# Four block sums of a second graph-attention projection, made by GpSimd instead of VectorE

## The chip, the cores and the metric

The kernel runs on one core of one Trainium2 chip. TensorE (PE in the profile) multiplies matrices, VectorE (DVE), ScalarE (ACT) and GpSimd (POOL) do the elementwise work, SyncE (SP) starts DMAs, and GpSimd starts those DMAs that add to what lies at their destination. Each engine works through its own queue in order; semaphores tie the queues together. The metric is the device time of one execution in microseconds (us).

## The reference

Two layers of graph attention with a residual, over 32 graphs of 512 nodes and 512 features:

```python
h = jnp.maximum(_layernorm(x, axis=-1), 0.0)
x = x + _L0_gnn_ref(adj, h, ...)

def gat_layer(x, mask, W, a_src, a_dst, bias, concat):
    xl = (x @ W).reshape(B, N, H, F)
    asrc = jnp.einsum('bnhf,hf->bnh', xl, a_src)
    adst = jnp.einsum('bnhf,hf->bnh', xl, a_dst)
    e = jax.nn.leaky_relu(asrc[:, :, None, :] + adst[:, None, :, :], NEG_SLOPE)
    e = jnp.where(mask[..., None], e, NEG_INF)
    attn = jax.nn.softmax(e, axis=1)
    out = jnp.einsum('bsdh,bshf->bdhf', attn, xl)
    ...
h = jax.nn.elu(gat_layer(x, mask, W1, ..., concat=True))    # 4 heads of 256
h = gat_layer(h, mask, W2, ..., concat=False)               # 1 head of 512
```

The matter here is the second layer's `x @ W2`: for each graph a product of 512 x 1024 with 1024 x 512 (and two more columns for the attention scores).

## The kernel before

Everything is float32. Each of the large products is made by Winograd's form of Strassen's method: both operands are cut into 2 x 2 blocks, a few sums of blocks are made, seven block products take the place of eight, and their results are added up on the way out of TensorE's banks (PSUM). `sums` (line 1008) makes the sums of the left operand:

- s1 = a21 + a22
- a21 = a11 - a21, written over the block a21
- s2 = s1 - a11
- s4 = a12 - s2

The products take their left operands from the table `left`: product 1 from a11, 2 from a12, 3 from s4, 4 from a22, 5 from s1, 6 from s2, 7 from the new a21.

For the second projection the left operand is `h1`, the output of the first layer, transposed: 8 tiles of 128 features by 512 nodes. `h1_blocks` (line 1039) cuts it with kh = KH = 4, so that a block is four 128 x 256 pieces, and each sum is one instruction on 128 partitions x 1024 elements. s1 and s2 go to the two halves of the buffer `hs`; there s4 has no place of its own and is written over s2. So in this case `sums` emits only the first three and leaves the fourth in `left[0]`; `sevens` (line 1058), which runs the seven products, calls it after the last product 6, the reader of s2. The other users of `sums` are the first projection (`ht_blocks`, kh = KQ = 2) and the last product of the second layer (`sums2`, line 1449, kh = KQ); they make sums of 128 x 512.

Product 5, 6 and so on are each made twice, once for each half of 128 rows. The order of `project2` (line 1399) is the table TWO: 1, 1, 2, 5, 6, 6, 2, 5, 7, 7, 3, 3, 4, 4, with the halves mixed.

`hs` is shared. Its first two of four pieces hold the sums of the first projection, the last two those of the last product of the second layer (`gather2`) and, one piece a head, those of the first layer's attention (`sums1`). Each `sums` for `h1` therefore has to wait until these have been read.

The main loop (line 1611) runs over 31 turns. A turn interleaves the work of several graphs: the attention product of the first layer of graph i+1, the first projection of graph i+2, the last product of graph i, and the second projection of graph i+1 with its four sums; one more set of these sums stands before the loop. So there are 32 sets, 128 instructions.

The order of the instructions on every engine is written by a planner, the class `Program` (line 223). The kernel's functions add jobs with an engine, a cost in us and the keys that they read and write. `order` (line 299) then goes through a modelled time: on each engine it takes the ready job of the lowest rank. A job's rank comes from the table PLACES by the job's number, moved on by a fixed amount each turn; it does not depend on the job's engine. On the queues that start DMAs (SP and POOL) a job, of any kind, is held back in the plan while the modelled backlog of transfers is over 3.5 us. On the chip each engine then follows the planned order, and semaphores make it wait where the plan was wrong.

GpSimd's queue holds, besides a few instructions at the start, the accumulating DMAs that add the mask to the attention scores (`accumulate`, line 522; two issues for each attention matrix, each for half of it) and one small power for the layer norm of a graph (line 770). ScalarE's exponential follows these DMAs, and the attention product on TensorE follows the exponential.

Of the kernel before, what the change touches and what calls it, by code (L numbers as in the profile page):

```python
# [378 lines left out]
def tile_gat(  # L379
# [36 lines left out]
    nc = tc.nc  # L416
# [12 lines left out]
    KH = FT // 2  # L429
# [81 lines left out]
    prog = Program()  # L511
# [4 lines left out]
    def dve(cost, reads, writes, f, *a, **k):  # L516
        prog.add("DVE", cost, reads, writes, lambda: f(*a, **k))  # L517

    def dma(size, reads, writes, to, at, cost=0.4):
        prog.add("SP", cost, reads, writes, lambda: nc.sync.dma_start(to, at), size)  # L520

# [85 lines left out]
    def weights1():  # L607
        for c in range(2):
            for r in range(2):
                for k in range(KQ):  # L610
                    row = (r * KQ + k) * P
                    ix = AT[r, c]
                    dma(
                        WLOAD, (), [("w1", ix, k)], w1_sb[:, ix, k, :, 2:],
                        w1[row : row + P, :].rearrange("p (j c f) -> p c j f", j=H // 2, c=2)[:, c],
                    )

    def scores1():

        vk, bc = ps_.take()  # L620
        for a, v in enumerate((as1, ad1)):
            for j in range(H // 2):
                dma(
                    XLOAD, (), [vk + ("v", a, j)], bc[:, 2 * a + j, :],
                    bass.AP(tensor=v.tensor, offset=v.offset + j * 2 * FH, ap=[[0, P], [1, 2 * FH]]),
                )
        for j in range(H // 2):
            for c in range(2):
                for a in range(2):
                    for r in range(2):  # L630
                        for k in range(KQ):
                            ix = AT[r, c]
                            jk, junk = xrs.take()
                            dve(
                                0.4, [vk + ("v", a, j), ("w1", ix, k)], [("w1s", ix, k, j), jk],
                                nc.vector.scalar_tensor_tensor,
                                junk[:, :FH], w1_sb[:, ix, k, j, 2:], 1.0,
                                bc[:, 2 * a + j, c * FH : (c + 1) * FH],
                                op0=OP.mult, op1=OP.mult, accum_out=w1_sb[:, ix, k, j, a : a + 1],
                            )  # L640
                            xrs.give(jk)
        for u in range(NT):
            for c in range(2):
                prog.alias(vk + (u, c), [vk + ("v", a, j) for a in range(2) for j in range(H // 2)])
        ps_.give(vk)

    def weights2():

        for (r, c), ix in AT.items():
            dma(  # L650
                2 * WLOAD, [("ht", 0, 0)], [("w2", ix)], w2_sb[:, ix, :, :M],
                w2[r * HF // 2 : (r + 1) * HF // 2, c * DO // 2 : (c + 1) * DO // 2].rearrange(
                    "(k p) f -> p k f", p=P
                ),
            )
# [342 lines left out]
    def hs_keys(i, k0, k1):  # L998
        return [("hs", i, k) for k in ((0,) if k0 == 0 else ()) + tuple(range(max(k0, KQ), k1))]
# [8 lines left out]
    def sums(blocks, kh, cost, at=0, place=None, keys=None):  # L1008

        a11, a12, a21, a22 = (blocks[r, c] for r, c in ((0, 0), (0, 1), (1, 0), (1, 1)))  # L1010
        if place is None:
            s1, s2 = ((hs[:, i, at : at + kh], hs_keys(i, at, at + kh)) for i in range(2))
            s4 = (hs4, [("hs", 2, 0), ("hs", 2, 1)]) if kh == KQ and at == 0 else s2
        else:
            s1, s2, s4 = (
                (place[:, i].rearrange("p (k m) -> p k m", m=M), keys) for i in range(3)
            )

        def op(f, to, u, v):
            dve(cost, u[1] + v[1], to[1], f, to[0], u[0], v[0])  # L1020

        op(nc.vector.tensor_add, s1, a21, a22)
        op(nc.vector.tensor_sub, a21, a11, a21)
        op(nc.vector.tensor_sub, s2, s1, a11)
        left = {1: a11, 2: a12, 3: s4, 4: a22, 5: s1, 6: s2, 7: a21}

        def last():
            op(nc.vector.tensor_sub, s4, a12, s2)

        if s4 is s2:  # L1030
            left[0] = last
        else:
            last()
        return left
# [414 lines left out]
    def sums2(b, soft, place=None, keys=None):  # L1449

        pk, p = soft.p[0]
        blocks = half_blocks(p, KQ, lambda r, c: p_keys(pk, (2 * c, 2 * c + 1), (r,)))
        left = sums(blocks, KQ, 0.602, KQ, place, keys)
        v = x2(b)
        b11, b12, b21, b22 = (
            (
                v[:, 2 * r : 2 * r + 2, c * W2H : (c + 1) * W2H],
                [x2_key(b, 2 * r + i, c) for i in range(2)],
            )
            for r in range(2) for c in range(2)  # L1460
        )
        t1, t2, t4 = (
            (t.rearrange("p (k f) -> p k f", f=M + 1), [k]) for k, t in (xs.take() for _ in range(3))
        )
        dve(TINY, (), t1[1], nc.vector.memset, t1[0][:, :, M:], 1.0)

        def op(to, a, c):
            dve(
                0.602, a[1] + c[1], to[1], nc.vector.tensor_sub,
                *(q[0][:, :, :M] for q in (to, a, c)),  # L1470
            )

        op(t1, b12, b11)
        op(t2, b22, t1)
        op(b12, b22, b12)
        op(t4, b21, t2)
        right = {1: b11, 2: b21, 3: b22, 4: t4, 5: t1, 6: t2, 7: b12}
        return left, {n: (q if n in (1, 2, 5) else q[:, :, :M], keys) for n, (q, keys) in right.items()}
# [91 lines left out]
    for n in SMALL:  # L1570
        sums_of_small_weights(n)
    left1 = sums(ht_blocks(), KQ, 0.602)
    s = S1[0] = Soft(0, 1, lambda z, i, zk: [zk + (0, c, t) for c in range(2) for t in range(NT)])
    for i in range(2):
# [27 lines left out]
    s.first(3)  # L1602
    sums_of_weights(w2_sb, lambda ix: [("w2", ix), ("w2s", ix)], 1.15)
    left2 = sums(h1_blocks(), KH, 1.135)
    run(project2(0, left2))
    for t in range(NT):
# [103 lines left out]
```

## Time and profile before

| | us |
|---|---|
| median of two runs | 2766.11 (2766.06 to 2766.17) |
| span of the profiled execution | 2767.6 |
| TensorE busy | 2742.4 |
| VectorE busy | 2558.2 |
| ScalarE busy | 2229.1 |
| GpSimd busy | 313.1 |

"Busy" counts the time in which at least one of the engine's instructions ran; instructions of one engine overlap a little, so one of 1.22 us on VectorE is followed by the next after 1.13. In a row of groups stand the line, the engine, the operation, the output and the inputs by their names, the shapes and the count, then the busy time, the mean of one in ns, and the idle time just before them with what ended it. A row of the timeline has the start in us from the start of the span, the length in us, then the same names; with "x8" the row holds eight instructions in a row. Line 531 is every matmul, 517 every VectorE instruction and 514 every ScalarE one, since helpers emit them; one tells them apart by the names. A 32-bit matmul shows as two rows, so one product of the second projection (four matmuls) has eight. A row "A <- B: 12.1, 1, 12.1" of the waits says that A waited for B for 12.1 us in all, once, 12.1 at the longest.

### The profile page before, as it was taken

The page shows a single profiled execution, that of the slowest core. Times are in us where ns is not written, and L with a number is a line of the kernel's source. Part 1 is how long each engine was busy: PE and PEld are TensorE (multiplying, and loading weights), DVE is VectorE, ACT ScalarE, POOL GpSimd, SP SyncE. Part 2 cuts the span into 40 slices and gives each one's busy share as a digit, 9 for nine tenths or more (in the row PEclk, how much of TensorE's full clock was granted, in tenths as well). Part 3 has the DMA queues.
Part 4 walks back from the last instruction along what each step waited for, and adds up shares of the span by engine and source line. Part 5 has one row for each costly group of instructions (what it writes and reads, how often), then busy time and mean ns, then how long its engine had stood idle before and what let it go on. Part 6 is the DMA issues. An engine that isn't in the chain of part 4 may idle for free. (4 is left out here: it accounts for less than half of the span.)

```text
span 2767.6 us, 42320 instructions
## 1 busy us (share of the span) xinstructions
PE 2742.4 (99%) x12924; PEld 2371.8 (86%) x12924; DVE 2558.2 (92%) x6732; ACT 2229.1 (81%) x4907; POOL 313.1 (11%) x356
## 2 busy tenths in 40 slices
PE   7999999999999999999999999999999999999999
PEld 6788888888888888888888888888888888888887
DVE  8999999999999999999999999999999999999996
ACT  5978888778887788877888877888778788788883
POOL 0110111101111111111011111111111111101110
PEclk9999999999999999999999999999999999999999
DMA  8657766667666667667676766766676767767563
GB/s 232 176 157 182 203 167 184 187 176 194 182 183 179 182 176 196 178 175 195 173 201 172 182 187 178 192 186 180 180 188 175 201 167 180 195 165 208 162 171 112
DMA packets 375864, 502.14 MB, mean 181 GB/s; under 512 B 222804, under 2 KB 227668, under 8 KB 375636
## 3 DMA queue, kind: packets, MB, share of 16 engines
q1 hardware_dynamic: 329844, 332.68, 42.4%
q0 software_dynamic: 45792, 166.74, 25.1%
q8 instruction: 103, 1.69, 0.3%
q14 instruction: 125, 1.02, 0.1%
HBM read 316.41 MB, written 51.31 MB: 133 GB/s over the span
## 5 line engine op out<-in xcount | busy, mean ns | idle before, releaser
L531 PE MATMUL mm<-w_sb,hs 128*128 128x257 f32 (+3 forms) x2908 | 667.0, 367 | 5.1 <-ACT mm L514 3.3
L531 PEld LDWEIGHTS mm<-w_sb,hs 128*128 128x128 f32 x2908 | 539.7, 190 | 87.7 <-ACT mm L514 6.7
L525 POOL DMA_DIRECT2D p<-dm x314 | 273.2, 875 | 2295.0 <-DVE p L517 764.3
L531 PE MATMUL mm<-w_sb,ht 128*128 128x258 f32 x2112 | 528.6, 382 | 2.7 <-ACT mm L514 2.5
L531 PE MATMUL mm<-p,xl 128*128 128x258 f32 (+1 forms) x1984 | 495.8, 383 | 0.1
L531 PE MATMUL mm<-w_sb,h 128*128 128x257 f32 x2056 | 477.8, 379 | 0.0
L517 DVE SCALAR_TENSOR_TENSOR p<-rr,z 128x512 f32<-128x512 f32 (+1 forms) x636 | 456.0, 742 | 2.4 <-DMA rr<-drr 2.4
L531 PEld LDWEIGHTS mm<-w_sb,ht 128*128 128x128 f32 x2112 | 393.7, 190 | 63.6 <-ACT mm L514 6.4
L514 ACT ACTIVATE p<-p,z 128x512 f32<-128x512 f32 (+1 forms) x636 | 433.4, 720 | 17.7 <-DVE p L517 12.4
L531 PEld LDWEIGHTS mm<-w_sb,h 128*128 128x128 f32 x2056 | 389.0, 189 | 58.4 <-ACT xl L514 0.5
L531 PEld LDWEIGHTS mm<-p,xl 128*128 128x128 f32 x1984 | 367.2, 190 | 52.7 <-issue 6.0
L514 ACT ACTIVATE mm<-mm 128x257 f32<-128x257 f32 (+2 forms) x498 | 169.8, 347 | 269.2 <-PE mm L531 236.2
L514 ACT ACTIVATE l<-as,z 128x512 f32<-128x512 f32 x516 | 354.4, 716 | 30.8 <-DMA as<-das 30.7
L514 ACT ACTIVATE l<-l,low 128x512 f32<-128x512 f32 x516 | 370.3, 721 | 7.6 <-DVE low L517 6.7
L517 DVE CUSTOM_DVE_ANT_1 l<-l,mt 128x512 f32<-128x512 f32 x516 | 346.2, 681 | 28.4 <-ACT l L514 27.4
L514 ACT ACTIVATE xl<-mm 128x258 f32<-128x258 f32 (+2 forms) x748 | 269.3, 382 | 91.4 <-PE mm L531 89.8
L514 ACT ACTIVATE h<-mm,b_sb 128x256 f32<-128x256 f32 (+1 forms) x504 | 231.0, 480 | 77.3 <-PE mm L531 76.6
L531 PE MATMUL mm<-t,hs 128*128 128x258 f32 (+1 forms) x992 | 246.1, 380 | 0.0
L517 DVE TENSOR_TENSOR xl<-xl,mm 128x258 f32<-128x258 f32 x372 | 155.3, 419 | 57.9 <-PE mm L531 48.3
L531 PEld LDWEIGHTS mm<-t,hs 128*128 128x128 f32 x992 | 185.8, 190 | 25.5 <-DVE t L517 0.2
L531 PE MATMUL mm<-xl,p 128*128 128x258 f32 (+2 forms) x752 | 189.7, 388 | 1.0 <-ACT h L514 0.6
L517 DVE SCALAR_TENSOR_TENSOR h<-xr,h 128x512 f32<-128x512 f32 x256 | 172.2, 683 | 6.1 <-ACT xr L514 6.1
(137 smaller groups left out, 3706.2 us busy)
## 6 DMA issues: line engine op xcount, KB each, us to landing
p<-dm POOLq DMA_DIRECT2D x314, 512.0 KB, 5.0
rr<-drr SPq DMA_DIRECT2D x159, 512.0 KB
x<-in_x_dram SPq DMA_DIRECT2D x129, 256.0 KB
adj<-in_adj_dram SPq DMA_DIRECT2D x128, 256.0 KB
as<-das SPq DMA_DIRECT2D x64, 512.0 KB
t<-in_x_dram SPq DMA_DIRECT2D x124, 256.0 KB
out_dram<-t SPq DMA_DIRECT2D x124, 256.0 KB
dm<-m SPq DMA_DIRECT2D x64, 256.0 KB
```

The source lines that it names most:

```text
L514: prog.add("ACT", cost, reads, writes, lambda: nc.scalar.activation(*a, **k))
L517: prog.add("DVE", cost, reads, writes, lambda: f(*a, **k))
L525: lambda: nc.gpsimd.dma_start(to, at, accum_op=OP.add), size,
L531: f(*a, **k)
```

## The change

The four sums of `h1` are added to the planner's list as jobs of GpSimd, with a cost of 2.4 us in place of 1.135, and are issued by `nc.gpsimd`. What they compute, their operands and their buffers are the same. The sums of 128 x 512 stay on VectorE. The number of jobs, and so every job's rank, is unchanged; the planner makes the order anew.

```diff
+    def pool(cost, reads, writes, f, *a, **k):
+        prog.add("POOL", cost, reads, writes, lambda: f(*a, **k))
+
...
+        eng = nc.gpsimd if kh == KH else nc.vector
+
         def op(f, to, u, v):
-            dve(cost, u[1] + v[1], to[1], f, to[0], u[0], v[0])
-
-        op(nc.vector.tensor_add, s1, a21, a22)
-        op(nc.vector.tensor_sub, a21, a11, a21)
-        op(nc.vector.tensor_sub, s2, s1, a11)
+            if kh == KH:
+                pool(2.4, u[1] + v[1], to[1], f, to[0], u[0], v[0])
+            else:
+                dve(cost, u[1] + v[1], to[1], f, to[0], u[0], v[0])
+
+        op(eng.tensor_add, s1, a21, a22)
+        op(eng.tensor_sub, a21, a11, a21)
+        op(eng.tensor_sub, s2, s1, a11)
         left = {1: a11, 2: a12, 3: s4, 4: a22, 5: s1, 6: s2, 7: a21}
 
         def last():
-            op(nc.vector.tensor_sub, s4, a12, s2)
+            op(eng.tensor_sub, s4, a12, s2)
```

## The prediction

> **What bounds the kernel now.** I read the busy table of the page first, then the waits of TensorE, then the busy time by stretches of one turn of the main loop, then the grouped instructions of VectorE and GpSimd, and last the timeline around the four sums of one turn.
>
> ```profile
> span 2767.6 us, 42320 instructions
> PE 2742.4 (99%) x12924; PEld 2371.8 (86%) x12924; DVE 2558.2 (92%) x6732; ACT 2229.1 (81%) x4907; POOL 313.1 (11%) x356
> ```
> ```profile
> PE mm L531 <- ACT x L514: 12.1, 1, 12.1
> PE mm L531 <- ACT mm L514: 5.8, 10, 1.2
> PE mm L531 <- DVE hs L517: 1.3, 1, 1.3
> ```
> ```profile
> core 0: us, PE busy (x) PEld busy (x) DVE busy (x) ACT busy (x) POOL busy (x), PEclk, DMA share, GB/s
> 1209.00:1293.70 84.70, 84.70 (x405) 73.99 (x404) 79.40 (x208) 69.78 (x155) 9.76 (x11) 1.00 0.70 184
> 1463.00:1547.70 84.70, 84.70 (x406) 73.99 (x405) 79.31 (x209) 69.73 (x155) 9.76 (x11) 1.00 0.70 184
> sum 338.70, PE 338.70 PEld 296.15 DVE 317.70 ACT 279.59 POOL 39.06; mean PE 84.67 PEld 74.04 DVE 79.42 ACT 69.90 POOL 9.76
> ```
>
> The reader is to see three things. TensorE (PE) is busy for the whole of a turn, 84.67 us of 84.67 (four turns in the sum row), at a granted clock of 1.00, and its largest waits add up to under 20 us in the whole run, 12.1 of them one wait at the start. So TensorE sets the time and the edit touches none of its work: what it can gain is at most TensorE's 2767.6 - 2742.4 = 25.2 us of idle time, 0.9%. VectorE (DVE) is close behind, 79.42 us, with 84.67 - 79.42 = 5.25 us of idle time in a turn. GpSimd (POOL) is busy for 9.76.
>
> The profiled execution spans 2767.6 us, 1.5 us above the median of the two runs, 2766.11; I sum against the span and take the 1.5 off at the end.
>
> **The change, part by part.** *Work taken from VectorE.* The four sums of each of 32 batches:
>
> ```profile
> L517 DVE TENSOR_TENSOR hs<-h,hs 128x1024 f32<-128x1024 f32 x32 | 39.1, 1222 | 3.6 <-PE mm L531 3.4
> L517 DVE TENSOR_TENSOR hs<-hs,h 128x1024 f32<-128x1024 f32 x32 | 39.0, 1219 | 0.3 <-PE mm L531 0.3
> L517 DVE TENSOR_TENSOR h<-h 128x1024 f32<-128x1024 f32 x32 | 38.9, 1217 | 0.0
> L517 DVE TENSOR_TENSOR hs<-h 128x1024 f32<-128x1024 f32 x32 | 38.6, 1207 | 0.1
> ```
>
> 128 instructions, 155.6 us, 4.86 a turn. On VectorE they lie beside TensorE's work, so their going is worth nothing by itself.
>
> *Work given to GpSimd.* No row has this operation on GpSimd at 1024 columns. The nearest:
>
> ```profile
> L525 POOL DMA_DIRECT2D p<-dm x314 | 273.2, 875 | 2295.0 <-DVE p L517 764.3 <-DVE t L517 596.2 <-PE mm L531 450.2
> L770 POOL TENSOR_TENSOR stats<-stats,half 128x4 f32<-128x4 f32 x32 | 35.9, 1120 | 97.9 <-DVE stats L517 96.2 <-ACT l L514 1.7
> masks.py:199 POOL TENSOR_SCALAR_AFFINE_SELECT identf<-identf 128x128 f32<-128x128 f32 x1 | 0.3, 292 | 0.1
> L1696 POOL MEMSET const-bfloat16-1.0<- 128x1 bf16 x1 | 0.1, 101 | 0.0
> ```
>
> The select reads one operand of 128 columns in 0.292 us, the memset of one column takes 0.101, so a read column costs about (292 - 101) / 128 = 1.5 ns. At 1024 columns that is 0.1 + 1.53 = 1.6 us if the second operand comes free, and 0.1 + 3.06 = 3.2 us if it costs as much again. I take the middle, 2.4 us (the number that the diff gives its planner too). Four of them make 9.6 us, and GpSimd goes from 9.76 to about 19.4 us of 84.67: it has the room. [...]
>
> *What of it reaches TensorE.* One turn on TensorE and on VectorE:
>
> ```profile
> 1391.00 1.89 PE L531 MATMUL mm<-xl,hs 128*128 128x256 f32 x8
> 1392.72 1.90 PE L531 MATMUL mm<-w_sb,h 128*128 128x257 f32 x8
> 1394.46 7.12 PE L531 MATMUL mm<-w_sb,hs 128*128 128x257 f32 x32
> 1401.42 3.64 PE L531 MATMUL mm<-w_sb,h 128*128 128x257 f32 x16
> 1404.90 3.64 PE L531 MATMUL mm<-w_sb,hs 128*128 128x257 f32 x16
> ```
> ```profile
> 1378.28 1.21 DVE L517 TENSOR_TENSOR hs<-h 128x1024 f32<-128x1024 f32 x1
> 1381.49 1.21 DVE L517 TENSOR_TENSOR h<-h 128x1024 f32<-128x1024 f32 x1
> ...
> 1394.07 1.22 DVE L517 TENSOR_TENSOR hs<-hs,h 128x1024 f32<-128x1024 f32 x1
> 1395.20 0.68 DVE L517 CUSTOM_DVE_ANT_1 l<-l,mt 128x512 f32<-128x512 f32 x1
> ...
> 1401.62 1.22 DVE L517 TENSOR_TENSOR hs<-h,hs 128x1024 f32<-128x1024 f32 x1
> 1402.76 0.69 DVE L517 TENSOR_TENSOR t<-p 128x512 f32<-128x512 f32 x1
> ...
> 1406.91 0.42 DVE L517 TENSOR_TENSOR xl<-xl,mm 128x257 f32<-128x257 f32 x1 [0.86 <-PE mm L531]
> ...
> 1411.43 0.69 DVE L517 TENSOR_TENSOR p<-p 128x512 f32<-128x512 f32 x1 [1.51 <-ACT p L514]
> ```
>
> A block product is eight matmul rows, 7.12 / 4 = 1.75 us each; the run of 32 on the sums (hs) is products 5, 5, 6, 6, the run of 16 after it the two of s4.
>
> - s1 and the new a21 have 1394.46 - 1379.5 = 15 us and 1401.42 - 1382.7 = 19 us until their first reader: 1.2 us more hides under other products. If that cover went, it would cost at most the lengthening, 1.2 each.
> - s2 can start when the last reader of its buffer ends at 1392.9 and is first read, as second or third of the run, at 1396.2 or 1397.9. Here VectorE began it only at 1394.07, behind other work, and ended at 1395.3. On GpSimd: 1392.9 + 0.2 + 2.4 = 1395.5, in time. With 3.2 us and an accumulating DMA (0.875) in front it would be 1397.2, up to 1.0 late.
> - s4 cannot start before the last product 6 ends, at 1401.4, since it overwrites s2. VectorE had it done at 1402.84, 2.06 us before 1404.90. On GpSimd it lasts 2.4 - 1.22 = 1.18 longer: 0.9 us of cover left at 2.4, nearly none at 3.2 (1.98 longer), a loss of 0.8 with 3.2 and a DMA of 0.875 in front. I take 0.1 a turn for s2 and s4 together, between 0 and 1.8.
>
> *VectorE beside a GpSimd sum.* This is the large unknown, since most of VectorE's long instructions read two operands of SBUF, as GpSimd's new ones do. The only GpSimd arithmetic in the loop:
>
> ```profile
> 1399.73 1.07 POOL L770 TENSOR_TENSOR stats<-stats,half 128x4 f32<-128x4 f32 x1 [1.35 <-DVE stats L517]
> ```
> ```profile
> 1399.48 0.82 DVE L517 TENSOR_TENSOR hs<-xl 128x256 f32<-128x256 f32 x2
> 1400.22 0.75 DVE L517 TENSOR_TENSOR xl<-xl 128x256 f32<-128x256 f32 x2
> ```
>
> During it VectorE's sums of two operands run at their usual pace: two in 0.82 us, two in 0.75. So this GpSimd instruction does not stop VectorE for its 1.07 us; but it reads four columns, not 1024. The bounds are therefore 0 (this row) and the whole sum (2.4 us) that VectorE stands still. I take half, 1.2 us a sum, as neither end has a near row: 4.8 us a turn come in place of the 4 x 1.13 = 4.5 us (1394.07 to 1395.20, start to next start) that left. VectorE's load then stays at 79.7 of 84.67, but in lumps: its evictions of TensorE's banks come up to 1 us late after a lump, until the gaps of 0.86 and 1.51 us take it up. For that I take 0.3 us of TensorE's time a turn, bounds 0 and the rival's figure below.
>
> *GpSimd's queue.* It holds 318 accumulating DMA issues (ten in most turns) and 32 small powers, in an order that the planner wrote; the sums are put between them. A DMA behind a sum is issued up to 2.4 us later, more if that sum waits for TensorE.
>
> ```profile
> 1394.66 0.86 POOL L525 DMA_DIRECT2D p<-dm  x1 [4.16 <-PE mm L531]
> 1397.52 0.86 POOL L525 DMA_DIRECT2D p<-dm  x1 [1.99 <-DVE p L517]
> ```
> ```profile
> ACT p L514 <- DMA p<-dm: 5.2, 8, 1.4
> ```
>
> The exponentials after these DMAs (ACT p) waited for them 5.2 us in the whole run, so there is slack, not known how much; the first of these two would wait for s2, about 1 us. I take 0.1 us a turn, bounds 0 and 1 x 2.4. SP's queue is passed by nothing. The planner makes the order anew with other readiness times from the same table of ranks; both signs are possible and I take 0.
>
> Sum: 0.1 + 0.3 + 0.1 = 0.5 us a turn, x 32 = 16 us; 2767.6 + 16 - 1.5 = 2782 us, **0.6% slower, within 2%**. Its own range: from nothing lost, 2766, to 1.1 us a turn, 2801.
>
> **The rivals.**
>
> *A: GpSimd's sums stop VectorE, and VectorE becomes the bound.* If every sum holds it for its whole 2.4 us, VectorE's turn is 79.42 - 4.5 + 9.6 = 84.5 us, as long as TensorE's. It then has no room for its own waits, now 5.25 a turn; if a third of these stay (1.75, the part that lateness can't absorb), a turn is 86.3 us, 1.6 more: 51 us in all, 2817. If s2 and s4 also start late because GpSimd waits for the VectorE instruction before them (0.69), it is 1 us a turn more, 2849. It decides from a hold of (4.5 + 5.25 - 1.75) / 4 = 2.0 us a sum. Against it: the row of the power above. For it: VectorE has no long gap between 1378 and 1404, where the sums lie. [...] The trace shows a GpSimd instruction that doesn't hold VectorE for its whole length, but none that streams.
>
> *B: VectorE's new room is worth something.* Without any hold it has 9.8 us of idle time a turn, and evictions come sooner. All of TensorE's idle time but the 12.1 us at the start is 13 us: 2766 - 13 = 2753. Against it: TensorE shows no gap in the turns.
>
> *C: the accumulating DMAs come late.* If the sums push both DMAs of one mask behind TensorE waits, ScalarE's exponentials and then TensorE stand: 2.4 us a turn, 77 us, 2843. Against it: GpSimd is idle for 75 us of each turn, and landing takes about 5 us with no wait today.
>
> **How the numbers follow.** Forecast 0.50, A 0.33, B 0.11, C 0.06. For this kernel about 2% is what a measurement of two runs tells from no change: 2711 to 2821. No case reaches 2711: faster 0.01. Slower is somewhat over half of A, most of C: 0.22 together. The rest, 0.77, is within. The range leaves out a quarter of B (0.03), a third of A (0.11: late s2 and s4) and C (0.06), 0.2 in all: 2752 to 2832.
>
> **What would show it.** Right: GpSimd rows of 128x1024 near 2.4 us, TensorE's new waits for GpSimd short and only before the products of s4 (or s2), VectorE's busy time about as before (2558.2 us), since the half hold gives back what left. Rival A: VectorE's 128x512 instructions with two operands lengthen (0.68 to 2 us) when a sum runs, its busy time rises, and TensorE waits for VectorE. Rival C: ScalarE's exponentials wait for DMAs. I am wrong if the sums take well over 3.2 us, or if VectorE's hold is complete.

## The result and the profile after

The changed kernel takes 3270.39 us (3267.88 to 3272.91, two runs) against 2766.11: a ratio of 1.181, 95% interval 1.179 to 1.183. It is 504 us slower, 15.8 us for each of the 32 batches. The forecast was 2782, within 2%.

The busy table of the page, the changed kernel:

```profile
span 3271.1 us, 42531 instructions
PE 2910.7 (89%) x12924; PEld 2440.2 (75%) x12924; DVE 2656.7 (81%) x6604; ACT 2275.7 (70%) x4907; POOL 631.5 (19%) x484
```

TensorE makes the same 12924 matmuls. Its idle time went from 25.2 to 3271.1 - 2910.7 = 360.4 us, 335 more, and its busy time from 2742.4 to 2910.7, 168 more. These two are the whole loss of 503.5 us between the two spans. So two questions follow: why TensorE waits, and why the same matmuls take longer.

The waits of TensorE and, last, those of ScalarE for the accumulating DMAs (us in all, times, longest), the changed kernel:

```profile
PE mm L534 <- ACT h L514: 152.4, 32, 7.3
PE mm L534 <- ACT xl L514: 86.2, 31, 5.0
PE mm L534 <- ACT mm L514: 42.6, 54, 2.6
PE mm L534 <- DVE t L517: 27.8, 14, 7.8
...
PE mm L534 <- POOL hs L520: 3.3, 2, 2.2
...
ACT p L514 <- DMA p<-dm: 18.1, 12, 4.6
```

TensorE hardly ever waits for GpSimd's sums: 3.3 us. The long waits are for ScalarE, which no line of the change touches, and the two largest come once a turn (32 and 31 times). ScalarE itself is less busy in share than before, 70% for 81%. So it is no engine at its limit; the experiments below show that it is work that stands in a bad order.

Three of the four rows of the sums on GpSimd, grouped by shape (count, busy us, mean ns, idle time before):

```profile
L520 POOL TENSOR_TENSOR h<-h 128x1024 f32<-128x1024 f32 x32 | 88.8, 2776 | 2.4
L520 POOL TENSOR_TENSOR hs<-h,hs 128x1024 f32<-128x1024 f32 x32 | 77.3, 2416 | 28.1 <-PE mm L534 19.2 <-ACT l L514 7.6 <-ACT p L514 1.2
L520 POOL TENSOR_TENSOR hs<-h 128x1024 f32<-128x1024 f32 x32 | 75.8, 2368 | 578.1 <-DVE z L517 284.3 <-ACT mm L514 212.1 <-PE mm L534 59.8
```

The sums take 2.37 to 2.78 us; 2.4 was forecast.

The longer matmuls are seen around one of TensorE's waits. The first two lines are of the busy time by stretches (the number behind the last pair with a count is the granted clock), the others of TensorE's timeline, the changed kernel:

```profile
1667.71:1674.54 6.83, 5.23 (x12) 3.82 (x13) 4.89 (x13) 3.09 (x8) 0.00 (x0) 0.50 0.64 175
1674.60:1681.00 6.40, 6.22 (x38) 5.55 (x37) 6.00 (x19) 3.82 (x10) 0.00 (x0) 1.00 0.57 159
```
```profile
1662.57 1.03 PE L534 MATMUL mm<-p,xl 128*128 128x256 f32 x4
1669.31 2.08 PE L534 MATMUL mm<-p,xl 128*128 128x258 f32 x4 [5.72 <-ACT h L514]
1671.26 2.09 PE L534 MATMUL mm<-w_sb,hs 128*128 128x258 f32 x4
...
1674.70 1.03 PE L534 MATMUL mm<-w_sb,ht 128*128 128x258 f32 x4
```

After a wait of 5.72 us four matmul rows take 2.08 us, where they took 1.03 before it; the granted clock is 0.50 for 6.83 us and then 1.00 again. The clock's record of this run holds 51 such stretches, nearly all of 3.41 us or a few times that, 318.6 us in all. TensorE was busy for 232.2 us of them; by an estimate from the rows above (2.08 us for 1.03) the full clock would have saved half of that, 116 of the 168 us. So a long wait like this one is paid once as idle time and then partly again. The other 52 us go with the number of breaks in TensorE's work, moments without any matmul: 22 before, 216 now. It comes to 0.27 us a break, and the first experiment below has 97 breaks more than before and 24.1 us more busy time, 0.25 each, without a low clock. Rows of matmuls overlap a little otherwise (1.03 us long, the next one 0.87 later); whether that is why was not shown. In the rows above an idle time of 5.72 us went with the half clock. Of the other stretches of this run, 15 began during an idle time of 3.2 us or within 8 us of its end, six had only shorter ones there, of 1.1 to 2.9 us, and one had none.

### The profile page after: what moved, and what is told of

Its sections match the earlier page's. It is cut to its first block, busy times and chain, and to the rows that moved or that the text cites. A ratio compares the mean times of both kernels' runs of the same rounds, so it can differ in the third digit from the quotient of the medians.

```text
span 3271.1 us, 42531 instructions
## 1 busy us (share of the span) xinstructions
PE 2910.7 (89%) x12924; PEld 2440.2 (75%) x12924; DVE 2656.7 (81%) x6604; ACT 2275.7 (70%) x4907; POOL 631.5 (19%) x484
## 3 DMA queue, kind: packets, MB, share of 16 engines
q14 instruction: 126, 1.03, 0.1%
## 4 chain that ended last, share of the span: by engine, by line
PE 48%; DVE 20%; ACT 19%; DMA 7%; issue 5%; POOL 0%; SPq 0%; DVEq 0%; ACTq 0%; POOLq 0%
PE mm L534 48%; ACT l L514 8%; DVE l L517 5%; DVE p L517 5%; ACT p L514 4%; DMA as<-das 3%; DVE xl L517 2%; DVE t L517 2%; DVE hs L517 2%; ACT xl L514 2%; ACT ht L514 2%; DMA p<-dm 1%; DVE z L517 1%; ACT xr L514 1%; ACT mm L514 1%
## 5 line engine op out<-in xcount | busy, mean ns | idle before, releaser
L534 PE MATMUL mm<-w_sb,hs 128*128 128x257 f32 (+3 forms) x2908 | 711.8, 385 | 17.2 <-ACT xl L514 6.5
L534 PE MATMUL mm<-p,xl 128*128 128x258 f32 (+1 forms) x1984 | 540.4, 407 | 157.6 <-ACT h L514 149.8
L534 PEld LDWEIGHTS mm<-w_sb,hs 128*128 128x128 f32 x2908 | 572.2, 200 | 112.3 <-ACT xl L514 8.7
L534 PE MATMUL mm<-w_sb,h 128*128 128x257 f32 x2056 | 514.5, 395 | 109.8 <-ACT xl L514 78.5
L534 PEld LDWEIGHTS mm<-p,xl 128*128 128x128 f32 x1984 | 392.7, 203 | 237.5 <-ACT h L514 162.5
L534 PEld LDWEIGHTS mm<-w_sb,h 128*128 128x128 f32 x2056 | 398.9, 196 | 191.5 <-ACT xl L514 88.5
L517 DVE CUSTOM_DVE_ANT_1 l<-l,mt 128x512 f32<-128x512 f32 x516 | 405.7, 805 | 69.8 <-ACT l L514 69.5
L514 ACT ACTIVATE p<-p,z 128x512 f32<-128x512 f32 (+1 forms) x636 | 426.4, 708 | 28.0 <-DMA p<-dm 18.1
L534 PE MATMUL mm<-t,hs 128*128 128x258 f32 (+1 forms) x992 | 256.8, 387 | 22.6 <-DVE t L517 21.0
L517 DVE SCALAR_TENSOR_TENSOR t<-mm,rs,t 128x256 f32<-128x256 f32 x360 | 167.7, 480 | 58.4 <-PE mm L534 54.6
```

What stands on the lines that cost most here:

```text
L514: prog.add("ACT", cost, reads, writes, lambda: nc.scalar.activation(*a, **k))
```

## The experiments

Three causes were to be told apart: the order of instructions that the planner writes (plan), VectorE being kept from its work while GpSimd's sums run (hold), and sums that end too late for TensorE (lateness).

**The engine alone.** The sums run on GpSimd, but the planner is told that they are VectorE jobs of 1.135 us, so all engines keep the order of before.

```diff
             if kh == KH:
-                pool(2.4, u[1] + v[1], to[1], f, to[0], u[0], v[0])
+                dve(cost, u[1] + v[1], to[1], f, to[0], u[0], v[0])
```

> The sums run on GpSimd, but the planner is still told that they are jobs of VectorE of 1.135 us, so that every engine's order is that of before. Theory plan (the new order costs most of the 504 us): 2766 to 2840, TensorE's waits small again. Theory hold (VectorE standing still beside GpSimd's sums costs most): 3150 or more, with VectorE's load up by about 200 us of held instructions, as in the changed kernel.

Measured: 2883.05 us, ratio 1.042 (1.040 to 1.043), 115.6 us more than before in the same session (2767.43). That lies between the two theories and in neither range: the new engine costs something real, but a quarter of the whole. The timeline of VectorE, then of GpSimd, then of TensorE in one turn of this run:

```profile
1520.89 1.31 DVE L517 TENSOR_SCALAR z<-xl 128x16 f32<-128x16 f32 x1
1522.12 0.47 DVE L517 SCALAR_TENSOR_TENSOR t<-mm,rs,t 128x256 f32<-128x256 f32 x1
1522.52 0.20 DVE L517 STREAM_TRANSPOSE as<-z 128x32 f32<-128x32 f32 x1
1522.64 2.51 DVE L517 CUSTOM_DVE_ANT_1 l<-l,mt 128x512 f32<-128x512 f32 x1
...
1525.09 0.47 DVE L517 SCALAR_TENSOR_TENSOR t<-mm,rs,t 128x256 f32<-128x256 f32 x1
```
```profile
1519.82 2.36 POOL L517 TENSOR_TENSOR hs<-h 128x1024 f32<-128x1024 f32 x1 [11.47 <-DVE low L517]
1522.25 2.35 POOL L517 TENSOR_TENSOR h<-h 128x1024 f32<-128x1024 f32 x1
```
```profile
1525.61 1.13 PE L534 MATMUL mm<-xl,p 128*128 128x256 f32 x4 [1.56 <-DVE t L517]
```

Read the ends. GpSimd's first sum runs to 1522.18, and VectorE's small z<-xl, 0.163 us on the average in the kernel before, ends at 1522.20. The second sum runs to 1524.60; l<-l,mt, which reads two operands of SBUF and starts at 1522.64, ends at 1525.15: it got its 0.6 us only after the sum. In between t<-mm,rs,t, whose first operand is in PSUM, and a transpose run at their usual length (0.47 and 0.20 us; 0.474 and 0.203 on the average before). The eviction behind l<-l,mt is late, and TensorE waits 1.56 us for its bank. The grouped rows of VectorE, first four of the kernel before, then those of this run:

```profile
L517 DVE SCALAR_TENSOR_TENSOR p<-rr,z 128x512 f32<-128x512 f32 x628 | 452.5, 746 | 1.2 <-DMA rr<-drr 1.2
L517 DVE CUSTOM_DVE_ANT_1 l<-l,mt 128x512 f32<-128x512 f32 x516 | 346.2, 681 | 28.4 <-ACT l L514 27.4 <-issue 0.3
L517 DVE SCALAR_TENSOR_TENSOR stats<-stats 128x4 f32<-128x4 f32 x32 | 5.2, 162 | 0.0
L517 DVE TENSOR_SCALAR z<-xl 128x16 f32<-128x16 f32 x62 | 10.1, 163 | 0.5 <-ACT xl L514 0.4
```
```profile
L517 DVE SCALAR_TENSOR_TENSOR p<-rr,z 128x512 f32<-128x512 f32 x628 | 504.3, 828 | 6.7 <-DMA rr<-drr 6.7
L517 DVE CUSTOM_DVE_ANT_1 l<-l,mt 128x512 f32<-128x512 f32 x516 | 398.8, 783 | 80.3 <-ACT l L514 80.0
L517 DVE SCALAR_TENSOR_TENSOR t<-mm,rs,t 128x256 f32<-128x256 f32 x360 | 164.9, 472 | 5.9 <-PE mm L534 1.9
L517 DVE SCALAR_TENSOR_TENSOR stats<-stats 128x4 f32<-128x4 f32 x32 | 65.3, 2041 | 0.0
L517 DVE TENSOR_SCALAR z<-xl 128x16 f32<-128x16 f32 x62 | 44.9, 725 | 3.8 <-ACT xl L514 1.3
```

Against the means of before (t<-mm,rs,t had 474 ns) the rows are longer by 82 x 628, 102 x 516, nothing, 1879 x 32 and 562 x 62 ns: 51 + 53 + 60 + 35 = 199 us, 1.55 us a sum, 6.2 us a turn. (In the changed kernel all rows together are 210 us longer.) And the waits of TensorE:

```profile
PE mm L534 <- DVE t L517: 44.7, 29, 1.6
PE mm L534 <- ACT mm L514: 33.3, 35, 1.1
...
PE mm L534 <- POOL hs L517: 5.2, 5, 1.8
```

5.2 us for GpSimd in all: lateness of the sums is nearly nothing even in this order.

**The order alone.** The reverse: the planner's order is that of the changed kernel, the sums run on VectorE.

```diff
-        eng = nc.gpsimd if kh == KH else nc.vector
+        eng = nc.vector
```

> The reverse: the planner is told of GpSimd jobs of 2.4 us, so that the order is that of the changed kernel, but VectorE makes the sums. Theory plan: 2980 to 3270 (the planner's own modelled end went from 2749 to 2978 us, 229 more; the rest would be where the chip falls behind the model). Theory hold: 2766 to 2850, since no GpSimd sum runs.

Measured: 3139.20 us, ratio 1.134 (1.132 to 1.136), 371.8 us more than before, without one sum on GpSimd. TensorE's largest wait is the one of the changed kernel:

```profile
PE mm L534 <- ACT h L514: 150.6, 32, 7.4
```

Order and engine, each alone, cost 371.8 + 115.6 = 487.4 of the 504.3 us. The remaining 17 were not pursued. The planner's 229 us more come near to what TensorE's idle time rose by in this run, from 25.2 to 3144.6 - 2875.3 = 269.3 us, so by 244 (in the run with 1.125 below it is 269 modelled and 208 measured). The rest of the loss is longer busy time of the same matmuls, which the model doesn't have.

**Is it this order, or any other order?** The kernel before with nothing changed but the cost of the sums that the planner is told; VectorE makes them as before.

```diff
-        left2 = sums(h1_blocks(), KH, 1.135)
+        left2 = sums(h1_blocks(), KH, 1.125)
```

(in both calls, and in the same way in the two runs that follow).

> The kernel before with one number changed: the planner's cost of each of the four sums is 1.125 instead of 1.135 us; all stays on VectorE. Theory plan, in its strong form (the rank table fits one set of costs and any other gives a worse order): about 3035 us (the planner's modelled end is 3018, and before the chip took 17 us more than the model). Theory hold, or a plan that is robust to small changes: 2766 to 2780.

Measured: 3092.75 us, ratio 1.118 (1.116 to 1.120): 325 us lost, with no instruction on another engine or of another size, and 58 us more than the strong form said. Two more values, a thousandth of a us to either side:

> The kernel before, the planner's cost of each sum 1.136 in place of 1.135. The planner's modelled end stays at 2749.3 us (2749.2 before). If the modelled end tells what an order is worth: 2763 to 2771. If any change of a cost harms: 3000 or more, as with 1.125.

> The same with 1.134, one thousandth of a us the other way. The planner's modelled end is 3002.8 us. If the modelled end tells what an order is worth: 3020 to 3100 (with 1.125 it was 3018.1 and the chip took 3092.75). If the harm with 1.125 came from something else than the order: 2763 to 2771.

Measured: 2767.66 us with 1.136 (ratio 1.000, 0.999 to 1.001) and 3084.83 with 1.134 (1.116, 1.111 to 1.120). The planner's own modelled end, which its class computes from its costs before any chip sees the program, for these and other values:

```
sums told as VectorE jobs:  cost 1.000  1.125  1.130  1.134  1.135  1.136  1.140  1.145  1.200
                    modelled end 2958   3018   3028   3003   2749   2749   2750   3004   2954
sums told as GpSimd jobs:   cost 0.2    1.0    1.8    2.4    2.8    3.4
                    modelled end 2988   2972   2931   2978   3003   2985
```

It is a narrow notch: 2749 to 2750 for 1.135 to 1.140, and 2930 to 3030 at every other value of the table. With 1.136 the order is that of 1.135 on every engine, so the program is the same, and its time too. With the sums told as GpSimd jobs the end is 2988 even at a cost of 0.2 us, so the length of the sums has nothing to do with it. Nor has the rule that holds back GpSimd's jobs while transfers are behind: with the sums freed of it, the planner of the changed kernel ends at 3040. In the modelled time of the changed kernel TensorE stands idle for 6.7 us in most stretches of 85 us, in that of before for 0.1. So the table of ranks fits the one sequence for which it was made. Not every change of a number leaves that sequence (1.136 doesn't), but taking 128 jobs off an engine's list did, at each of the six costs.

**Which sums hold, and whether lateness plays a part.** Both in the order of before, the diff of the first experiment and in addition two of the four sums back on VectorE:

```diff
-        op(eng.tensor_sub, s2, s1, a11)
+        op(nc.vector.tensor_sub, s2, s1, a11)
...
-            op(eng.tensor_sub, s4, a12, s2)
+            op(nc.vector.tensor_sub, s4, a12, s2)
```

> The order of before again, and only s1 and the new a21 on GpSimd; s2 and s4 on VectorE. These two have 15 and 19 us until their first reader, so they can't come late. Theory hold (GpSimd's sums keep VectorE from its work): VectorE stands still by some 1.6 us a sum beside them, and the wait of 1.56 us a turn that TensorE has for a VectorE eviction (DVE t) when the order of before runs with all four on GpSimd stays: 2800 to 2835. Theory lateness (sums on GpSimd end too late for TensorE): 2762 to 2775.

and the other two in the same way:

> The order of before, and only s2 and s4, the two with little cover, on GpSimd. Theory hold: about the other half of the 116 us that all four cost in this order, 2805 to 2845. Theory lateness: all of it, 2865 to 2885, with TensorE waiting for GpSimd in the list of waits.

Measured: 2830.36 us (ratio 1.023, 1.022 to 1.025) and 2829.80 (1.023, 1.021 to 1.025), 62.7 and 62.2 us more than before; together 125, against 116 for all four at once. The sums with 15 and 19 us of cover cost as much as those with little: it is the hold. The waits of TensorE, first with s1 and a21 on GpSimd, then with s2 and s4, show hardly any for GpSimd:

```profile
PE mm L534 <- DVE t L517: 46.4, 29, 1.6
...
PE mm L534 <- POOL hs L517: 1.1, 1, 1.1
```
```profile
PE mm L534 <- ACT mm L514: 37.7, 37, 1.3
...
PE mm L534 <- POOL hs L517: 2.4, 3, 0.9
```

The first pair costs TensorE the late VectorE evictions (DVE t) of the first experiment, the second pair late evictions by ScalarE (ACT mm). How the hold gets there is seen in one turn of the second run, on GpSimd, VectorE, ScalarE and TensorE:

```profile
1515.79 2.75 POOL L517 TENSOR_TENSOR hs<-h,hs 128x1024 f32<-128x1024 f32 x1 [0.17 <-PE mm L534]
```
```profile
1516.25 2.31 DVE L517 SCALAR_TENSOR_TENSOR stats<-stats 128x4 f32<-128x4 f32 x1
```
```profile
1518.59 1.52 ACT L514 ACTIVATE x<-x,stats 128x512 f32<-128x512 f32 x2 [1.68 <-DVE stats L517]
```
```profile
1528.20 1.13 PE L534 MATMUL mm<-t,hs 128*128 128x256 f32 x4 [1.29 <-ACT mm L514]
```

VectorE's small stats<-stats, 0.162 us before, ends at 1518.56 with the sum (1518.54). ScalarE stands 1.68 us for it, then works without a gap up to the eviction mm<-mm, and TensorE waits 1.29 us for that one.

**What of the sum holds VectorE.** In the order of before, GpSimd in place of each sum first only writes zeros, then copies one operand. Both leave the second layer's sums out.

```diff
-                pool(2.4, u[1] + v[1], to[1], f, to[0], u[0], v[0])
+                dve(cost, u[1] + v[1], to[1], nc.gpsimd.memset, to[0], 0.0)
```
```diff
-                pool(2.4, u[1] + v[1], to[1], f, to[0], u[0], v[0])
+                dve(cost, u[1] + v[1], to[1], nc.gpsimd.tensor_copy, to[0], u[0])
```

> The order of before; in place of each of the four sums GpSimd writes zeros to its output (128x1024) and reads nothing. The second layer's sums are left out by this. From the memset of 128 columns (0.204 us) and of one (0.1) it lasts some 0.95 us. Theory: VectorE is held by what GpSimd reads. Then VectorE's instructions of two operands keep their length beside it, and the time is 2750 to 2775. Rival: any GpSimd instruction that streams holds VectorE; then the rows beside it lengthen by up to 0.95 us, and the time is 2785 to 2830.

> The order of before; in place of each of the four sums GpSimd copies one operand to the output (128x1024), so that it reads one operand and not two. The second layer's sums are left out by this. Some 1.6 us each by the row of the select. Theory hold by reading: VectorE's rows beside it lengthen to about the end of the copy, less than with the sums in proportion to its length: 2790 to 2840. If only two read operands hold VectorE: 2750 to 2775.

Measured: 2767.88 us (1.000, 0.999 to 1.001) and 2769.11 (1.001, 1.000 to 1.002). First VectorE and GpSimd beside a writing instruction:

```profile
1401.30 0.95 POOL L517 MEMSET hs<- 128x1024 f32 x1 [1.41 <-PE mm L534]
```
```profile
1401.57 0.69 DVE L517 TENSOR_TENSOR t<-p 128x512 f32<-128x512 f32 x1 [0.31 <-ACT p L514]
```

then beside a copying one:

```profile
1400.40 1.04 POOL L517 COPY hs<-h 128x1024 f32<-128x1024 f32 x1 [0.90 <-PE mm L534]
```
```profile
1400.94 1.04 DVE L517 TENSOR_TENSOR t<-p 128x512 f32<-128x512 f32 x1 [0.62 <-ACT p L514]
```

The same t<-p keeps its 0.69 us beside the write and is stretched to 1.04, half a us past the copy's end, beside the read. The means of three rows of VectorE with two SBUF operands say the same: t<-p 683 ns before, 684 with the write and 798 with the copy; l<-l,mt 681, 681 and 708; p<-rr,z 746, 745 and 761 ns. So in these runs the copy, which reads, held such instructions, and the write didn't. The time doesn't follow here, though, and the expectation of 2790 to 2840 for the copy was wrong: a copy lasted 1.04 us and not 1.6, and the hold was short. All of VectorE's rows together are 39 us longer, 0.3 us a copy, while VectorE is rid of 1.13 us of work a sum. That this room covers the hold is likely, but no run tests it by itself. In both runs TensorE's products still depend on what GpSimd writes, and nothing is lost; so the handing over of the blocks from GpSimd to TensorE isn't what costs the 116 us.

## Why the prediction was wrong, step by step

- **The step that failed** is the last clause of GpSimd's queue: "The planner makes the order anew with other readiness times from the same table of ranks; both signs are possible and I take 0." It should have been 371.8 / 32 = 11.6 us a turn. Nor was it one of the rivals: all of them argued about the old order with other lengths in it. The order was taken as if it would stay, though the text itself said that it wouldn't. What "both signs" overlooked was in the first rows quoted: with TensorE at 84.67 of 84.67 us in each turn there was next to nothing for another order to win (25.2 us of idle time in the whole run), so another order could cost nothing or lose, and how much was open.
- **The hold of VectorE** was sized at 1.2 us a sum, half of the sum; measured 1.55 in the order of before. That is 6.2 us a turn in place of 4.8. It was the stop of rival A, complete for the instructions held in the turns shown: they ended 0.02 to 0.55 us after the sum. That the mean is less than a whole sum fits the turn of the first experiment, where VectorE worked on for 0.4 us beside the second sum (1522.25 to 1522.64) until it came to an instruction that was held. The row that was taken as the lower bound, the power of 1.07 us, misled: VectorE's sums ran beside it at full pace, two in 0.82 us and two in 0.75. The power reads four columns and not 1024; whether that is why was not shown.
- **What the hold costs TensorE** was put at 0.3 us a turn; the first experiment shows 115.6 / 32 = 3.6. Rival A would have it come from a full VectorE. VectorE was not full (2624.0 of 2882.3 us busy in that run), and the mean hold stayed under the 2.0 us from which that rival reckons a loss. The path was the one that the prediction named, evictions that come late after a lump. But single instructions were held by about 2 us (l<-l,mt 2.51 for 0.68, stats<-stats 2.31 for 0.16) where the prediction had evictions at most 1 us late, the gaps did not take it up, and the late evictions of ScalarE behind a held VectorE instruction were not counted. With the right size here the forecast would have been about 2882 (2766 + 116) even in the old order, not 2782; the range ended at 2832.
- **The length of a sum**, 2.4 us, was right (2.37 to 2.78 on the average; 2.36 and 2.35 in the turn shown), though the way to it was luck: the row of the select overstated a read column, since a copy of 1024 columns took 1.04 us.
- **The cover of s1, a21, s2 and s4** (0.1 a turn, 3.2 us in all) was right: TensorE's waits for GpSimd are 5.2 us in the order of before, for which it was worked out, and 3.3 in the changed kernel.
- **The accumulating DMAs** (0.1 a turn; rival C): ScalarE's exponentials waited 18.1 us for them in all, 0.6 a turn, on 12 occasions; in the order of before they waited 1.9. Rival C did not happen.
- **Rival B**, a gain from VectorE's new room, has no substance: with zeros in place of the sums VectorE's busy time fell to 2440.2 us and it was hardly held (its rows were about 17 us longer in all), and the time was that of before, 2767.88.
- **The clock** was in no step: the rows of before show 1.00 in every turn. In the changed kernel it adds 116 us of slower matmuls to 335 us of waiting, so a wait cost a third more than the sum reckoned, and half as much again with the 52 us at the breaks.

## What to carry to other kernels

Where a greedy planner works from a table of ranks fitted to one set of jobs and costs, price the new order before the moved instruction: run the planner, or keep the order and move only the engine. And when an engine is full in every turn, an unknown change of order can hardly win and may lose much. Beside a VectorE with hardly any gaps a long GpSimd instruction can be paid for by VectorE: here a sum of 2.4 us took away 1.13 us of work and put 1.55 us of standing still in its place, while a copy of 1.04 us cost nothing that the time shows.

## What the runs showed of the hardware

- Writing alone, GpSimd held one kind of VectorE instruction. With the zeros, the row of z<-xl, a scalar multiplication of 16 columns from SBUF to SBUF with one tensor operand, rose from 163 to 444 ns, while l<-l,mt stayed at 681:

```profile
L517 DVE TENSOR_SCALAR z<-xl 128x16 f32<-128x16 f32 x62 | 27.5, 444 | 5.1 <-ACT xl L514 2.5
L517 DVE CUSTOM_DVE_ANT_1 l<-l,mt 128x512 f32<-128x512 f32 x516 | 346.4, 681 | 34.4 <-ACT l L514 31.9
```

- In the first experiment a held VectorE instruction showed in the profile as a long busy one (l<-l,mt 2.51 us for 0.68), not as a wait: VectorE's busy time rose from 2558.2 to 2624.0 us with 128 instructions fewer. A count of busy time alone would call it more work.
- In the turns shown a GpSimd copy of 128x1024 took 1.04 us (1.06 to 1.10 on the average), a difference of two operands 2.35, 2.3 times as long.
- In the changed kernel the granted clock of TensorE fell to 0.50 in stretches of 3.41 us and multiples, up to 13.65, most of them around long idle times: in 44 of its 54 idle times of over 3 us between matmuls such a stretch began during it or within 8 us of its end. With the order of before and the sums on GpSimd, TensorE was idle for 2882.3 - 2766.5 = 115.8 us, 13.1 of them at the start and the rest in waits of at most 1.8, and the mean clock stayed at 1.0.
